# One attention kernel on one core: where the row shifts stand in front of the scores

## The chip, the cores and the metric

The kernel runs on one core of one Trainium2 chip. Its time is the device time of the whole launch in microseconds (us). Before the change it is 4384.06 us, the median of three runs that lie between 4382.21 and 4387.28.

## What is computed

The input x has 4 sequences of 2048 tokens with 512 features. Two branches work on the layer-normalised x, and both are added to x.

```python
xn  = layernorm(x)
qkv = xn @ w_qkv                       # 16 heads of 32
q, k = irfft(rfft(q) * mask), irfft(rfft(k) * mask)
out = softmax(q @ k.T / sqrt(32)) @ v  # per sequence and head
y1  = out @ w_out + b_out
y2  = top-1 experts: 8 experts with 100 places each, one shared weight w_expert
return x + y1 + y2
```

The attention branch is nearly all of the work. The softmax is over 2048 keys for each of 2048 queries, 16 heads and 4 sequences.

## The kernel before

**Tiling.** Four heads make a group, so there are 16 pairs of sequence and group (k in the code). Each has four blocks of 512 queries (n), and each block has 16 tiles of 128 keys (j). One tile of keys is a **half** (two of them, even and odd, make a window). There are 16 x 4 x 16 = 1024 halves. In a half the scores of four heads are computed, keys on the partitions and queries along the row, in two **rounds** u of two heads each. A head has 32 features, so its matmul takes 32 of the 128 rows of the array: round 0 uses the row groups that begin at 0 and 32, round 1 those at 64 and 96.

**The shift.** The softmax needs the maximum over the keys, which lie across partitions here. So the maximum is taken ahead of time in a second product with queries on the partitions: `max_matmuls` (line 465) multiplies q and k once more, and `max_reduce` (line 477) lets VectorE (DVE) reduce two banks to maxima. The list `stream` (line 454) orders these products 40 pieces ahead of the scores that need them; each round of a half takes one piece, always of the other two heads, so that with the scores of the round all four row groups are at work. At the end of a block the negated maxima go through a transpose (`max_close`), are split into three bf16 parts (`max_split`, GpSimd) and sent by SyncE into `negm`. `shift` (line 619) adds them up in PSUM with a matmul of three ones per head, in bf16; `scores` (line 608) then accumulates the product of keys and queries into the same bank. ScalarE (ACT) takes the exponential of each of the four banks, and in the next half `products` (line 635) multiplies the result with v, four heads side by side in the columns of the array; DVE adds that to the running sum `num`. The sums of exponentials are gathered from pairs of tiles by an accumulating transfer (`pair`) and by GpSimd (`add_to`).

**Banks.** PSUM is one array of eight banks. `bank()` (line 118) and `next(turns)` hand them out strictly in turn. A half takes nine: four for scores, four for maxima, one for `products`. Whoever gets a bank waits until the last reader of what it held is done.

**Order.** Every engine runs its instructions in the order in which the program emits them (`InOrder`, line 72, pins it). The main loop (lines 950 to 1005) emits for each half: shifts, then in each round the maximum matmuls, scores, exponentials and the reduce, then the products of the half before, then the steps that `agenda` holds for this half. The agenda is planned ahead of the loop: projections of the next pair, transposes, the router, the experts, and the closing steps of the block before (row sums, eight reciprocals, output projection). `at` (line 801) puts a step into a half and adds its planned cost on PE to `costs` (line 798), `spread` (line 805) places a list of steps so that the costs are even, and line 934 adds 0.5 where `max_close` falls. A step of DVE, ACT or GpSimd alone is planned with cost 0.

For pieces of the maximum beyond the last (the last 20 halves) the rounds hold only scores.

Of the kernel before, what the change touches and what calls it, by code (L numbers as in the profile page):

```python
# [102 lines left out]
def attention_and_top1_experts(ctx: ExitStack, tc: tile.TileContext, a: dict, out: bass.AP):  # L103
# [14 lines left out]
    def bank():  # L118

        return array[:, next(turns), :]  # L120
# [36 lines left out]
    def chunk(name):  # L157
        tag, bufs = ("y", 1) if name == "y" else ("xs", None)
        return chunks.tile([P, TQ, DM], F32, tag=tag, name=name, bufs=bufs)

    def probs(odd):

        name = "odd" if odd else "even"
        return probs_pool.tile([P, 2, 2, QB], F32, tag=name, name=name, bufs=3 if odd else 5)
# [300 lines left out]
    def max_matmuls(item, half):  # L465
        k, n, m, t, u = item
        for h in range(2):
            at = DH * (2 * u + h)
            on.tensor.matmul(
                array[:, half[h], :],  # L470
                lhsT=qs[k, n][at : at + DH, t * P : (t + 1) * P],
                rhs=ks[k][at : at + DH, m * QB : (m + 1) * QB],
                start=True,
                stop=True,
            )

    def max_reduce(item, half):
        k, n, m, t, u = item
        if (k, n) not in parts:
            parts[k, n] = small.tile([P, HG, TQ, NQ], F32, name="part", bufs=2)  # L480
        for heads, scored in joined(*half):
            part = parts[k, n][:, 2 * u : 2 * u + 2, t, m]
            on.vector.reduce_max(part[:, heads], scored, axis=AX.X)
        if (m, t, u) == (NQ - 1, TQ - 1, 0):
            full_blocks.append((k, n))
# [3 lines left out]
    def max_negate(k, n):  # L489
        negs[k, n] = small.tile([P, HG * TQ], F32, name="neg")  # L490
        part = parts.pop((k, n)).rearrange("p h t m -> p (h t) m")
        on.vector.tensor_reduce(negs[k, n], part, AX.X, ALU.max, negate=True)

    def max_close(k, n):

        pn = bank()[0 : HG * TQ, 0:P]
        on.tensor.matmul(pn, lhsT=negs.pop((k, n)), rhs=ident, start=True, stop=True)
        rest = small.tile([HG * TQ, P], F32, name="rest")
        row = small.tile([HG * TQ, 3, P], BF16, name="row", bufs=2)
        on.scalar.copy(row[:, 0, :], pn)  # L500
        on.scalar.copy(rest, pn)
        closed[k, n] = rest, row
# [3 lines left out]
    def max_split(k, n):  # L506

        rest, row = closed.pop((k, n))
        for i in (1, 2):
            on.gpsimd.tensor_tensor(rest, rest, row[:, i - 1, :], ALU.subtract)  # L510
            on.gpsimd.tensor_copy(row[:, i, :], rest)
        negms[k, n] = qkv.tile([P, QB], BF16, tag="negm", name="negm", bufs=3)
        for i in range(3):
            on.sync.dma_start(out=negms[k, n][i::DH, :], in_=row[:, i, :])
# [93 lines left out]
    def scores(k, n, j, u, half):  # L608
        for h in range(2):
            at = DH * (2 * u + h)  # L610
            on.tensor.matmul(
                half[h],
                lhsT=ks[k][at : at + DH, j * P : (j + 1) * P],
                rhs=qs[k, n][at : at + DH, :],
                start=False,
                stop=True,
            )

    def shift(k, n, u, half):
        for h in range(2):  # L620
            at = DH * (2 * u + h)
            on.tensor.matmul(
                half[h],
                lhsT=ones_b[at : at + 3, :],
                rhs=negms[k, n][at : at + 3, :],
                start=True,
                stop=False,
            )
# [6 lines left out]
    def products(k, n, j, tile, num):  # L635
        po = bank()
        four_heads(po, lambda at: vs[k][:, j, at], tile, start=True, stop=True)
        if j == 0:
            on.scalar.copy(num, po)
        else:  # L640
            on.vector.tensor_tensor(num, num, po, ALU.add)
# [156 lines left out]
    costs = [0.0] * len(agenda)  # L798
# [140 lines left out]
    def pair(first, second):  # L939
        on.gpsimd.dma_start(out=first, in_=second, accum_op=ALU.add)  # L940

    def add_to(tile, sum_before, engine):
        for u in range(2):
            engine.tensor_tensor(tile[:, u], tile[:, u], sum_before[:, u], ALU.add)
# [3 lines left out]
    window = 0  # L948
    maxima = stream[MAX_AHEAD:]
    for k in range(B * NG):  # L950
        for n in range(NQ):
            num = work.tile([P, QB], F32, tag="num", name="num")
            tiles = {}
            for w in range(NW):
                even, odd = w * WIN, w * WIN + 1
                if window in splits:
                    max_split(*splits.pop(window))
                for step in heads[2 * window]:
                    step()
                if window in pairs:  # L960
                    pair(*pairs.pop(window))
                if window in adds:
                    add_to(*adds.pop(window))
                for j in (even, odd):
                    tiles[j] = probs(j == odd)

                    halves = [(bank(), bank()) for u in range(2)]
                    for u in range(2):
                        shift(k, n, u, halves[u])
                    for u in range(2):  # L970
                        half = halves[u]

                        mate = maxima.pop(0) if maxima else None
                        if mate:
                            mh = next(turns), next(turns)
                            max_matmuls(mate, mh)
                        scores(k, n, j, u, half)
                        for h in range(2):
                            on.scalar.activation(tiles[j][:, u, h, :], half[h], AF.Exp, scale=SCALE)
                        if mate:  # L980
                            max_reduce(mate, mh)
                    while full_blocks:
                        filled = full_blocks.pop(0)
                        max_negate(*filled)
                        full[window + 1] = filled
                    if left:
                        products(*left)
                    left = k, n, j, tiles[j], num
                    if j == even and window in full:
                        splits[window + 1] = full.pop(window)  # L990
                        max_close(*splits[window + 1])
                    for step in agenda[2 * window + (j == odd)]:
                        step()
                last = (k, n) == (B * NG - 1, NQ - 1)
                if not last or w < NW - 2:
                    pairs[window + 1] = tiles[even], tiles[odd]
                    if 0 < w:

                        due, engine = (2, on.gpsimd) if maxima else (3, on.vector)
                        adds[window + due] = tiles[even], tiles[even - WIN], engine  # L1000
                if last and w == NW - 2:
                    y = chunk("xs")
                    on.sync.dma_start(out=y, in_=o[B - 1, n])
                window += 1
            ended[k, n] = num, tiles[NT - WIN]
# [39 lines left out]
```

## Time and profile before

| | us |
|---|---|
| three runs, median | 4384.06 |
| profiled execution | 4377.26 |
| its span, first to last instruction | 4375.4 |
| DVE busy | 3345.9 |
| GpSimd (POOL) busy | 2942.7 |
| ACT busy | 2653.9 |
| DVE's wait for PE before reduces of `part` | 921.0 |
| shift matmuls, mean of one | 0.385 |
| score and maximum matmuls, mean of one pass | 0.59 |

The granted TensorE clock was 0.993 over the span. All steps are recorded at one line, L83, that of the helper that pins the order, so rows are told apart by the tiles they write and read: `array<-negm,ones_b` is the shift, `array<-q,k` the scores, `array<-k,q` the maximum matmuls, `array<-even,v` and `array<-odd,v` the products, `array<-xnT,wg` a projection, `array<-wo,ot` the output projection. In a timeline row the first number is the start in us from the span's beginning, the second the length; x4 means that four instructions are merged into the row. PEld are weight loads. Each f32 matmul appears as two instructions. The ends of matmuls are modelled: they hold the way through the array as well, so that neighbours overlap in the rows, and the distance from start to start is the better measure.

### The profile page before, as it was taken

The page shows a single profiled execution, that of the slowest core. Times are in us where ns is not written, and L with a number is a line of the kernel's source. Part 1 is how long each engine was busy: PE and PEld are TensorE (multiplying, and loading weights), DVE is VectorE, ACT ScalarE, POOL GpSimd, SP SyncE. Part 2 cuts the span into 40 slices and gives each one's busy share as a digit, 9 for nine tenths or more (in the row PEclk, how much of TensorE's full clock was granted, in tenths as well). Part 3 has the DMA queues.
Part 4 walks back from the last instruction along what each step waited for, and adds up shares of the span by engine and source line. Part 5 has one row for each costly group of instructions (what it writes and reads, how often), then busy time and mean ns, then how long its engine had stood idle before and what let it go on. Part 6 is the DMA issues. An engine that isn't in the chain of part 4 may idle for free. (4 is left out here: it accounts for less than half of the span.)

```text
span 4375.4 us, 129380 instructions
## 1 busy us (share of the span) xinstructions
PE 4281.4 (98%) x56110; PEld 1906.5 (44%) x56110; DVE 3345.9 (76%) x4059; ACT 2653.9 (61%) x5527; POOL 2942.7 (67%) x2009
## 2 busy tenths in 40 slices
PE   8999999989999999999999999998999999999998
PEld 4444444434444444443544444443444443544432
DVE  6777778867777777886777877787777877677786
ACT  3556666666666666657566666665756665566665
POOL 0677666666776666776677766767668676677773
PEclk9999999999999999999999999999999999999999
DMA  4777877887777778788677777788877886778788
GB/s 116 182 140 153 158 151 164 190 186 146 141 150 154 153 152 159 168 191 184 128 156 153 154 151 154 160 173 191 165 137 153 166 165 130 142 156 162 153 158 171
DMA packets 161379, 690.71 MB, mean 158 GB/s; under 512 B 25302, under 2 KB 30584, under 8 KB 95528
## 3 DMA queue, kind: packets, MB, share of 16 engines
q0 software_dynamic: 110432, 605.83, 70.7%
q1 hardware_dynamic: 49200, 76.09, 5.6%
q8 instruction: 439, 7.19, 0.6%
q14 instruction: 132, 1.08, 0.1%
q10 hardware_dynamic: 1176, 0.52, 0.1%
HBM read 59.27 MB, written 88.96 MB: 34 GB/s over the span
## 5 line engine op out<-in xcount | busy, mean ns | idle before, releaser
L83 DVE TENSOR_REDUCE part<-array 128x2 f32<-128x1024 f32 (+1 forms) x2297 | 2427.8, 1104 | 924.4 <-PE array L83 921.0
L83 POOL TENSOR_TENSOR even<-even 128x1024 f32<-128x1024 f32 x876 | 2124.4, 2530 | 473.8 <-DMA even<-odd 473.1
L83 PE MATMUL array<-q,k 32*128 32x512 f32 x8192 | 1936.3, 593 | 0.0
L83 PE MATMUL array<-k,q 32*128 32x512 f32 x8192 | 1930.3, 591 | 2.2 <-DVE part L83 1.5
L83 ACT ACTIVATE even<-array 128x512 f32<-128x512 f32 x2048 | 1058.1, 604 | 496.0 <-PE array L83 488.2
L83 ACT ACTIVATE odd<-array 128x512 f32<-128x512 f32 x2048 | 1057.4, 603 | 485.2 <-PE array L83 387.2
L83 PEld LDWEIGHTS array<-k,q 32*128 32x128 f32 x8192 | 820.0, 187 | 423.3 <-issue 270.7
L83 POOL DMA_DIRECT2D even<-odd x510 | 468.5, 919 | 681.5 <-ACT odd L83 624.9
L83 PEld LDWEIGHTS array<-q,k 32*128 32x128 f32 x8192 | 762.5, 184 | 39.3 <-issue 17.1
L83 DVE TENSOR_TENSOR num<-num,array 128x512 f32<-128x512 f32 x960 | 649.8, 677 | 25.0 <-PE array L83 18.7
L83 PE MATMUL array<-even,v 128*32 128x512 f32 x4096 | 545.6, 605 | 14.2 <-ACT odd L83 14.2
L83 PE MATMUL array<-odd,v 128*32 128x512 f32 x4096 | 546.9, 605 | 7.4 <-ACT even L83 7.4
L83 PEld LDWEIGHTS array<-xnT,wg 128*32 128x32 f32 x15808 | 446.7, 110 | 242.5 <-issue 125.8
L83 PE MATMUL array<-xnT,wg 128*32 128x128 f32 (+1 forms) x15808 | 527.3, 277 | 0.7 <-ACT xnT L83 0.7
L83 PE MATMUL array<-negm,ones_b 3*128 3x512 bf16 x4096 | 440.7, 385 | 13.0 <-DVE num L83 7.6
L83 PEld LDWEIGHTS <-ones_b 3*128 3x128 bf16 x4096 | 111.7, 91 | 466.7 <-issue 466.7
L83 PE MATMUL array<-wo,ot 128*32 128x512 f32 x2048 | 268.9, 598 | 37.0 <-POOL ot L83 36.9
L83 PEld LDWEIGHTS array<-wg,xnT 128*32 128x32 f32 x8192 | 231.9, 110 | 124.6 <-issue 62.8
L83 DVE RECIPROCAL factor<-den 128x64 f32<-128x64 f32 x504 | 273.9, 544 | 0.0
L83 PE MATMUL array<-wg,xnT 128*32 128x128 f32 x8192 | 263.8, 273 | 0.0
L83 PEld LDWEIGHTS array<-even,v 128*32 128x32 f32 x4096 | 80.7, 108 | 408.6 <-ACT odd L83 400.4
L83 PEld LDWEIGHTS array<-odd,v 128*32 128x32 f32 x4096 | 81.0, 108 | 407.8 <-ACT even L83 398.5
(126 smaller groups left out, 1588.8 us busy)
## 6 DMA issues: line engine op xcount, KB each, us to landing
even<-odd POOLq DMA_DIRECT2D x510, 1024.0 KB, 8.1
out_dram<-y POOLq DMA_DIRECT2D x63, 1024.0 KB, 10.1
xs<-in_L_attn_x_dram SPq DMA_DIRECT2D x30, 1024.0 KB
out_dram<-xs SPq DMA_DIRECT2D x16, 1024.0 KB
wg<-wd SPq DMA_DIRECT2D x15, 768.0 KB
wo<-in_L_attn_w_out_dram SPq DMA_DIRECT2D x16, 256.0 KB
negm<-row SPq DMA_DIRECT2D x192, 4.0 KB
even<-in_L_attn_w_qkv_dram SPq DMA_DIRECT2D x2, 512.0 KB
```

The lines of the kernel that those rows point to most:

```text
L83: done = act(*args, **kwargs)
```

## The change

In a half whose predecessor holds agenda steps with a cost on PE, the shifts of both rounds stay ahead of everything, as before. In the other halves each round's two shifts are emitted at the head of that round. With them the two banks of round 1's scores are taken from the turn at that point, after the two banks of round 0's maxima, and not before them.

```diff
-                    halves = [(bank(), bank()) for u in range(2)]
-                    for u in range(2):
+
+                    together = costs[2 * window + (j == odd) - 1] > 0
+                    halves = [(bank(), bank()) for u in range(2)] if together else []
+                    for u in range(2 * together):
                         shift(k, n, u, halves[u])
                     for u in range(2):
+                        if not together:
+                            halves.append((bank(), bank()))
+                            shift(k, n, u, halves[u])
                         half = halves[u]
 
                         mate = maxima.pop(0) if maxima else None
```

So on PE the order of a half of the second kind is: two shifts, two maximum matmuls, two scores, two shifts, two maximum matmuls, two scores.

## The prediction

> **What bounds the kernel now.** I read the page's first lines first, then the waits of PE, then the timeline of single halves.
>
> ```profile
> PE 4281.4 (98%) x56110; PEld 1906.5 (44%) x56110; DVE 3345.9 (76%) x4059; ACT 2653.9 (61%) x5527; POOL 2942.7 (67%) x2009
> ```
>
> PE bounds. Only 94 us of the span of 4375.4 have no matmul in flight, but matmul ends are modelled, so a short stall inside a half does not show as idle time. Starts in the timeline do show it. This is an ordinary half, with a projection piece as its other work (PE rows alone):
>
> ```profile
> 1501.17 0.40 PE L83 MATMUL array<-negm,ones_b 3*128 3x512 bf16 x4
> 1501.40 0.59 PE L83 MATMUL array<-q,k 32*128 32x512 f32 x2
> 1501.41 0.59 PE L83 MATMUL array<-k,q 32*128 32x512 f32 x2
> ...
> 1503.23 1.06 PE L83 MATMUL array<-odd,v 128*32 128x512 f32 x8
> 1504.11 1.06 PE L83 MATMUL array<-xnT,wg 128*32 128x128 f32 x32
> 1505.10 0.39 PE L83 MATMUL array<-negm,ones_b 3*128 3x512 bf16 x4
> ```
>
> Shifts take 0.23 (start to start). Scores (q,k) and maximum matmuls (k,q) run on four row groups at once; each f32 matmul is two passes of 0.43 (the next start at 1501.83). Four passes (two rounds) end about 1503.12, 0.10 later the products start, 0.88 later the projection. A half without other work would take 0.23 + 1.72 + 0.10 + 1.0 = 3.05. Now the end of a block, where halves hold no other work:
>
> ```profile
> 625.12 0.40 PE L83 MATMUL array<-negm,ones_b 3*128 3x512 bf16 x4
> ...
> 626.46 2.36 DVE L83 TENSOR_REDUCE part<-array 128x2 f32<-128x1024 f32 x2 [0.75 <-PE array L83]
> 626.55 2.06 ACT L83 ACTIVATE odd<-array 128x512 f32<-128x512 f32 x4 [1.01 <-PE array L83]
> 627.22 1.07 PE L83 MATMUL array<-even,v 128*32 128x512 f32 x8
> 628.22 0.84 PE L83 MATMUL array<-negm,ones_b 3*128 3x512 bf16 x4
> 628.67 0.09 PEld L83 LDWEIGHTS <-ones_b 3*128 3x128 bf16 x1 [0.35 <-issue]
> ...
> 628.90 1.09 PE L83 MATMUL array<-k,q 32*128 32x512 f32 x3
> ...
> 630.79 1.07 PE L83 MATMUL array<-odd,v 128*32 128x512 f32 x8
> 631.79 0.85 PE L83 MATMUL array<-negm,ones_b 3*128 3x512 bf16 x4
> ```
>
> The half at 625.12 takes 3.10, the one at 628.22 takes 3.57. Its first two shifts start at 628.22; the third only at 628.67, when the last of ACT's four exponentials (626.55 + 2.06 = 628.61) has freed its bank; scores and maxima start at 628.88, when DVE's second reduce (626.46 + 2.36 = 628.82) has freed the next. Without these waits they would start at 628.45: 0.43 lost, and 0.1 more because weight loads come late (a score matmul shows 0.69 in place of 0.59). The half at 631.79 repeats it.
>
> **The change, part by part.** It adds and removes no instruction on PE. From the planned costs I count 83 of 1024 halves whose predecessor has cost 0: only these split their shifts. 36 follow a half that still leads with all four (a first split half: that at 628.22), 47 follow another split one (a later: that at 631.79). All others keep their order.
>
> Banks: a half takes nine of eight in turn, so each place takes the bank that the next place held one half earlier. Now, the order is S0 S0 S1 S1 M0 M0 M1 M1 P (scores, maxima of either round, products), and the opening shifts wait for all four exponentials and a reduce, the first maxima for the last reduce. Split, it is S0 S0 M0 M0 S1 S1 M1 M1 P.
>
> First split half: after a leading half, M0's first bank is the one that S1's last exponential frees: 628.67. Queued behind that wait is the score pair of round 0, so it starts there too. The chain of the row groups 64 and 96 is then 628.67 + 0.10 (weights no longer loaded behind a shift) + 0.86 maxima + 0.21 shift + 0.86 scores = 630.70. Before, the products at 630.79 say 630.69. So **0 us**; ends -0.1 (weights hidden after all) and +0.1.
>
> Later split half, at 631.79: nothing that opens it waits any more (the third exponential is done by 631.5: round 1's scores start at 629.84, their second pass 0.43 later, and 0.72 after that, as for 629.41 and 630.13 in the trace, ACT can start). 631.79 + 0.01 + 0.10 + 0.86 = 632.76; shift to 632.97. A new last wait comes: M1's second bank holds the products of 630.79, and DVE adds them 1.51 later (627.22 to 628.73), at 632.30, done about 632.98. Round 1's scores are queued behind this wait. 632.98 + 0.10 + 0.86 + 0.10 drain = products at 634.05, against 634.36 in the trace: **0.30 saved**; ends 0.2 and 0.45 (the add hidden).
>
> Later split halves in a row, where DVE also has a reciprocal each half: its own work is 2.27 (two reduces) + 0.59 (add) + 0.56 (reciprocal) = 3.42, against periods of 3.48 to 3.61 now. DVE is next: **0.13 saved**; ends 0 and 0.2.
>
> Count of the 47: 19 of the first kind (14 block ends, 4 before row sums, 1 early), 17 with reciprocals, 3 where the half then stands for 11 us behind POOL's chain at a stage change (PE's waits on POOL `ot` reach 11.1), 8 in the tail without maxima. The last two kinds give 0: there the banks and matmuls are the same, in another queue order. Sum: 19 x 0.30 + 17 x 0.13 = **7.9 us**.
>
> The queues of ACT, POOL and SP keep their order; DVE gets 8 fewer split reduces (two of 683 for one of 1220: 1.2 us in all, hidden). The last halves of a block have DVE, ACT and POOL free enough: POOL's two adds and pair transfer take about 5.9 of a 6.8 us window. If that cover is gone, a pair landing late holds an ACT tile, and the 7.9 shrinks.
>
> **A rule that speaks against it.** The Trainium skill (TensorE: Matmul & The Clock Gate, Part 3, What overlaps and what doesn't) says that matmuls start and end strictly in program order, only weight loads being pulled ahead, and those only into another row group. Then the second shift pair would stand behind the second pass of the scores ahead of it: in the 11 split halves without maxima up to 0.64 each, 7 us; and its weight load, into a row group still at work, 0.09 in each of 83, 7.5 us. The change would gain nothing. The trace disagrees twice. At 1501.40 the scores start before the maxima, which are ahead of them in the program: rows 0 and 32 came free first. And here a shift in one pair of row groups runs beside scores in the other:
>
> ```profile
> 4160.64 0.09 PEld L83 LDWEIGHTS <-ones_b 3*128 3x128 bf16 x1 [0.35 <-issue]
> ...
> 4160.66 0.70 PE L83 MATMUL array<-q,k 32*128 32x512 f32 x2
> ...
> 4160.86 0.61 PE L83 MATMUL array<-k,q 32*128 32x512 f32 x2
> ```
>
> The second shift pair started at 4160.64, scores on the other rows at 4160.66, maxima on the shift's own rows 0.22 after it. bf16 and f32 mix and the row groups queue apart. I take the row: 0. Not shown anywhere is a bf16 weight load while f32 matmuls stream; the nearest row is an f32 load at 1501.83 into rows whose second pass had just begun, at no cost.
>
> **The rivals.**
> - Whole relief: the add is never late and loads stay hidden. 28 first halves x 0.5 + 19 x 0.5 + 17 x 0.15 = 26 us, 4358. Against it: the banks above, counted by hand.
> - Absorbed: waits of ACT tiles on pair transfers (18.0 us now), DVE or tail take it back: 4384, within 4 of it. For it: two halves of the tail take 5.25 and 9.44 where 2.18 is usual, held by DVE and transfers.
> - Slower: the bf16 weight load in mid-half cannot run beside f32 matmuls and drains the row groups. Place: the second shift pair of all 83. Price: 0.2 in 36 later halves, 0.15 in 33 first ones, 1.1 in 11 without maxima (half of it absorbed by stalls there): 7 + 5 + 6 to 13, less 7.9, is 10 to 17 slower, about 4396. It decides once a split half pays over 7.9 / 83 = 0.095. For it: now all 4096 loads of ones_b stand where nothing else runs; against it: 628.22, where three such loads overlap running shifts.
> - That the order does not change can be excluded: the built program shows the moved shifts.
>
> **Numbers.** The profiled execution took 4377.26 (span 4375.4), 6.8 below the median of three, 4384.06; the sum of waits saved is taken off either: 4369.4 profiled, 4376.2 for the median. Chances: forecast 0.58 (4372 to 4381), whole relief 0.09, absorbed 0.13, slower 0.20. 0.2% (8.8 us) is about what a measurement can tell from no change; the forecast lies just inside, so 0.27 of its 0.58 is faster. Faster 0.36, same 0.44, slower 0.20. The range 4368 to 4396 leaves out whole relief and half of slower.
>
> **What will tell.** Right: first split halves stay at 3.57, later ones take about 3.27 (3.42 with reciprocals), their second shift pair starting 0.9 to 1.0 after the first while scores run, and the DVE add ending just before the last maximum. Wrong: first split halves near 3.1 (whole relief); a pause before the second shift pair, with longer halves in the tail (slower); shorter halves at an unchanged total (absorbed).

## The result, and the profile after

The changed kernel takes 4376.22 us (median of 18 runs, 4371.10 to 4379.97), the kernel before 4383.86 us (18 runs, 4380.91 to 4387.41). The ratio is 0.9981, 95% interval 0.9974 to 0.9987: about 8 us faster, real, and just below the 0.2% that the prediction took as its bound. The profiled execution took 4371.16 us (before 4377.26), its span is 4369.4 us (before 4375.4), at the same granted clock of 0.993. So the total is the predicted one. The terms of its sum are not, as the halves below show.

The busy times of the engines, from the top of the page of the changed kernel:

```profile
PE 4279.1 (98%) x56110; PEld 1911.6 (44%) x56110; DVE 3344.5 (77%) x4051; ACT 2658.5 (61%) x5527; POOL 2942.0 (67%) x2009
```

This line hardly tells the two kernels apart: PE has the same 56110 matmuls and is 2.3 us less busy, and DVE has 4051 instructions where it had 4059, the 8 split reduces less that were forecast. What changed is where matmuls start. This is the end of the same block as in the prediction, from the timeline of the changed kernel (start in us, length, engine, operation; the bracket is the idle time before it and what ended it):

```profile
626.35 0.39 PE L83 MATMUL array<-negm,ones_b 3*128 3x512 bf16 x2
626.79 0.19 PEld L83 LDWEIGHTS array<-k,q 32*128 32x128 f32 x2 [0.35 <-ACT odd L83]
...
627.75 0.38 PE L83 MATMUL array<-negm,ones_b 3*128 3x512 bf16 x2
...
628.93 1.06 PE L83 MATMUL array<-odd,v 128*32 128x512 f32 x8
...
629.92 0.39 PE L83 MATMUL array<-negm,ones_b 3*128 3x512 bf16 x2
...
630.26 0.68 DVE L83 TENSOR_TENSOR num<-num,array 128x512 f32<-128x512 f32 x1
630.46 0.59 PE L83 MATMUL array<-k,q 32*128 32x512 f32 x2
630.46 0.10 PEld L83 LDWEIGHTS <-ones_b 3*128 3x128 bf16 x2
...
630.89 0.38 PE L83 MATMUL array<-negm,ones_b 3*128 3x512 bf16 x2
630.99 0.18 PEld L83 LDWEIGHTS array<-k,q 32*128 32x128 f32 x1 [0.22 <-DVE num L83]
...
631.01 0.67 PE L83 MATMUL array<-k,q 32*128 32x512 f32 x2
...
632.07 1.07 PE L83 MATMUL array<-even,v 128*32 128x512 f32 x8
...
633.92 0.39 PE L83 MATMUL array<-negm,ones_b 3*128 3x512 bf16 x4
```

The half at 626.35 is a first split half. Its two opening shifts start at once, and then the maxima wait 0.44 for a bank that ACT's last exponential frees (626.79). It takes 3.57 to the next half, as before. The half at 629.92 is a later one. Nothing waits at its head; its second shift pair starts 0.97 after the first, while scores and maxima of round 0 run. The one wait left is that of round 1's maxima for DVE's add of the products (630.26, released at 630.99). It takes 4.00, output piece included, where the same half took 4.43 before.

I measured all 1024 halves in this way, from the first shift of one to the first shift of the next, in both profiled executions. Positive is saved, and a split half is "first" or "later" as in the prediction:

| halves | number | predicted, us | measured, us | each (measured) |
|---|---|---|---|---|
| first split, with maxima | 33 | 0 | +1.0 | median -0.01 |
| later split | 19 | 5.7 | +8.1 | mean +0.43 |
| later split, with a reciprocal each | 17 | 2.2 | +4.8 | mean +0.28 |
| later split, stage change | 3 | 0 | +0.7 | mixed |
| split, tail without maxima | 11 | 0 | -4.5 | one of them -6.6 |
| all that still lead, and the prologue | 941 | 0 | -4.1 | singly within 1.2 |
| sum | | 7.9 | 6.0 | |

The rows of split halves repeat in other traces. The row of the 941 others does not: up to half 976, where three of the kernels below (e5, e8, e10) are the same as the changed one, the halves that lead are between 3.2 us slower (changed kernel) and 1.4 faster (e5) than in the one trace of the kernel before, with the prologue counted in. So most of its -4.1 is scatter between executions (1.2 of it is half 1008, below).

Up to the end of half 1003 the changed kernel is 11.4 us ahead, after half 1006 12.0, after half 1007 only 5.4, and at the end 6.0. Half 1007 (counted from 0) is one in which PE comes to the output projection of the block before, and that needs `ot` from POOL. PE's timeline there, with the shifts of half 1008, of the changed kernel and then of the kernel before:

```profile
4295.88 1.93 PE L83 MATMUL array<-wo,ot 128*32 128x512 f32 x8 [4.84 <-POOL ot L83]
4297.75 0.61 PE L83 MATMUL array<-negm,ones_b 3*128 3x512 bf16 x4
```

```profile
4302.16 1.06 PE L83 MATMUL array<-wo,ot 128*32 128x512 f32 x8 [0.53 <-POOL ot L83]
4303.16 0.40 PE L83 MATMUL array<-negm,ones_b 3*128 3x512 bf16 x4
```

PE stood 4.84 us for it, in place of 0.53. Over the whole span PE's wait on `ot` grew from 36.9 to 41.1 us. The rows show a second cost: behind the stall the same eight matmuls take 1.87 to the next shift, and 1.00 before. The clock says why. These are the engines' busy times over halves 992 to 1007, changed kernel and then before; the third number from the end of a line is the granted TensorE clock:

```profile
4238.49:4297.75 59.26, 54.26 (x463) 18.53 (x461) 44.06 (x54) 36.91 (x72) 43.10 (x29) 0.96 0.83 163
```

```profile
4248.24:4303.16 54.92, 53.92 (x462) 18.29 (x459) 42.70 (x52) 36.70 (x72) 39.13 (x28) 1.00 0.82 160
```

In the changed kernel's trace the granted clock is 0.50 from 4293.4 to 4300.2, which covers the end of half 1007 and most of half 1008 (4.19 in place of 3.04). Of the 7.7 us that these two halves lose, 4.3 are the longer wait for `ot`, 2.0 the matmuls at half the clock behind it, and 1.4 lie ahead of it, where ACT waits 1.60 for a tile that POOL's add still holds (4287.88). So in these two executions the change won about 12 us and gave about 6 of them back in one place.

### The profile page after: what moved, and what is told of

It reads as the page before. It is cut to its first block, busy times and chain, and to the rows that moved or that the text cites. A ratio compares the mean times of both kernels' runs of the same rounds, so it can differ in the third digit from the quotient of the medians.

```text
span 4369.4 us, 129421 instructions
## 1 busy us (share of the span) xinstructions
PE 4279.1 (98%) x56110; PEld 1911.6 (44%) x56110; DVE 3344.5 (77%) x4051; ACT 2658.5 (61%) x5527; POOL 2942.0 (67%) x2009
## 3 DMA queue, kind: packets, MB, share of 16 engines
q14 instruction: 133, 1.09, 0.1%
## 5 line engine op out<-in xcount | busy, mean ns | idle before, releaser
L83 PE MATMUL array<-wo,ot 128*32 128x512 f32 x2048 | 269.7, 600 | 41.2 <-POOL ot L83 41.1
```

What stands on the lines that cost most here:

```text
L83: done = act(*args, **kwargs)
```

## The experiments

All twelve are variants of the changed kernel, each timed in five rounds against the kernel before on the same chip; a ratio is to that. The chips differ from run to run, so kernels are compared by ratios. "Cost" of a half in the code is the planned cost of its agenda steps on PE.

### The order of the queue alone, and the order of the banks alone

The first kernel keeps the split emission but takes all four score banks ahead of it, in the old order. The second takes the banks in the new order but emits all four shifts ahead.

```diff
 # e1_order_only
-                    halves = [(bank(), bank()) for u in range(2)] if together else []
+                    halves = [(bank(), bank()) for u in range(2)]
...
-                            halves.append((bank(), bank()))
                             shift(k, n, u, halves[u])
 # e2_banks_only
-                    for u in range(2 * together):
+                    halves = [(bank(), bank())]
+                    early_mh = None
+                    if not together and maxima:
+                        early_mh = next(turns), next(turns)
+                    halves.append((bank(), bank()))
+                    for u in range(2):
                         shift(k, n, u, halves[u])
```

> Splits the shifts in the same 83 halves, but all four score banks are taken up front as before the change. Theory (the gain comes from the bank order): with the old order the second bank of the first maxima is still the one that DVE's last reduce frees (0.65 after the half's natural start), and now round 0's scores and round 1's shifts queue behind it, so each of the 69 split halves with maxima is some 0.2 longer than before the change: about 14 us slower, 4398 where the kernel before has 4384. Rival (the gain comes from the queue order, the second shift pair no longer standing in front): as the change, about 8 us faster, 4376.

> All four shifts lead in every half as before the change; only the banks are handed out in the order of the change (round 0's scores, round 0's maxima, round 1's scores, round 1's maxima) in the 83 halves. Theory (it needs both, bank order and queue order): the fourth shift now waits for DVE's last reduce, so later split halves stay at about 3.6 and the first ones grow by up to 0.2; total between the kernel before and 14 us slower, 4384 to 4398. Rival (bank order alone is enough): about 8 us faster, 4376.

Measured: order alone 4378.92 us, ratio 1.0002 (0.9993 to 1.0010); banks alone 4381.47 us, ratio 1.0009 (1.0001 to 1.0018). With the order alone first split halves became 0.21 longer (3.57 to 3.78), 4.8 us in all. Of the 19 later ones an extra 0.2 was expected too; 8 of them kept their length (4.43 mostly), 10 became 0.20 to 0.34 shorter (4.40 to 4.20 mostly) and one longer, together 2.1 us saved. With the banks alone the two kinds became 0.10 and 0.11 longer. So neither part gains anything in the total. The full gain of a later half needs both: the shift of round 1 must stand behind round 0 in the queue, and round 0's maxima must get the banks that come free early. That moving the shifts alone brings the gain is refuted by the first kernel, though it relieves half of the later halves in part; that the bank turn alone does is refuted by the second.

### Which bank holds the first split halves

The prediction's step for them was that M0's first bank (M0 are the maxima of round 0, S1 the scores of round 1) is the one of S1's last exponential. In this kernel a first split half gives the fourth and fifth bank of its turn to M0, the third and sixth to S1; all else is the change.

```diff
+                    here = 2 * window + (j == odd)
+                    swap = here > 1 and not together and costs[here - 2] > 0 and len(maxima) > 1
...
+                    if swap:
+                        halves.append((bank(), bank()))
+                        b3, b4, b5, b6 = (next(turns) for _ in range(4))
+                        early_mh = b4, b5
+                        halves.append((array[:, b3, :], array[:, b6, :]))
```

> As the change, but in each split half that follows a leading one round 0's maxima take the fourth and fifth bank and round 1's scores the third and sixth, so that the first maxima no longer wait for the bank of the last exponential. Theory (that bank is why these 33 halves saved nothing): they fall from 3.58 to about 3.15, and 25 to 28 of them keep it, so 10 to 12 us more than the change: about 4365. Rival (they are held by something else, DVE's reduce or weight loads): they stay at 3.58 and the time at 4376.

Measured: 4360.42 us, ratio 0.9963 (0.9949 to 0.9976), 17.5 us off the span of before. The first split half of the same block in this kernel's timeline:

```profile
626.12 0.39 PE L83 MATMUL array<-negm,ones_b 3*128 3x512 bf16 x2
626.12 0.70 PE L83 MATMUL array<-k,q 32*128 32x512 f32 x2
...
628.42 1.06 PE L83 MATMUL array<-odd,v 128*32 128x512 f32 x8
629.42 0.39 PE L83 MATMUL array<-negm,ones_b 3*128 3x512 bf16 x2
```

The maxima start with the shifts, 0.44 earlier than in the changed kernel, and the half takes 3.30 in place of 3.57. So that bank did hold it. Part of the 0.44 comes back at once: the maxima of round 1 now wait (627.21, 0.13 behind the shift), and the later half that follows saves 0.31 in place of 0.43.

### The price of a split where nothing is gained

Every half splits its shifts, so 941 more than in the change.

```diff
-                    together = costs[2 * window + (j == odd) - 1] > 0
+                    together = False
```

> Every half splits its shifts, whatever the half ahead of it holds. Theory (in a split half the first maxima start with a weight load of 0.10 that no shift covers, and nothing is won where other work gives the banks time): some 900 halves pay 0.10 each, 80 to 100 us slower, 4465 to 4485, while the 33 first split halves become later ones and win 10. Rival (the load is hidden, splitting is free and helps every half): at most 4376, or lower.

Measured: 4420.76 us, ratio 1.0100 (1.0085 to 1.0116), about 43 us slower than before and half of the 80 to 100 expected. Halves that hold a piece of cost 1 became 0.083 longer (642 of them), of cost 2 0.093 (189), without a wait to relieve. A half with a projection piece, as in the prediction's first window, from this kernel's timeline:

```profile
1516.51 0.39 PE L83 MATMUL array<-negm,ones_b 3*128 3x512 bf16 x2
1516.51 0.70 PE L83 MATMUL array<-k,q 32*128 32x512 f32 x2
...
1517.04 0.59 PE L83 MATMUL array<-k,q 32*128 32x512 f32 x2
...
1518.65 1.06 PE L83 MATMUL array<-odd,v 128*32 128x512 f32 x8
```

From the first shift to the products it is 2.14, against 2.06 for the half at 1501.17 before. The first maxima start at once but show 0.70 in place of 0.59: their f32 weight load now has no shift in front of it to hide behind. Their second passes start 0.53 behind the first (1517.04), where 0.43 is usual, and this 0.10 makes up the price; a pause at the bf16 weight load, which the rival "slower" needs, does not show. In the profiled execution the halves that led before cost 56 us in all up to the tail (less than 932 times 0.083, since some others of them became shorter), and the first split halves save 0.40 each, 13 us: their predecessor, split too, no longer leaves the late bank.

### Splitting also the half ahead, and leading again near the end

Three kernels put the last run of short halves back (all halves from 998 on lead), to see whether that run starves POOL and makes half 1007 long: the change, the swap of banks, and a split of every half that holds no work or follows one that holds none.

```diff
 # e5_not_last
-                    together = costs[2 * window + (j == odd) - 1] > 0
+                    together = costs[2 * window + (j == odd) - 1] > 0 or 2 * window >= 998
 # e6_swap_not_last: the swap of e3, and
+                    together = costs[here - 1] > 0 or here >= 998
 # e7_either_not_last
+                    here = 2 * window + (j == odd)
+                    together = (costs[here - 1] > 0 and costs[here] > 0) or here >= 998
```

> As the change, but from half 998 on all four shifts lead again, as before the change. Up to there the change had saved 10.1 us by half starts; behind it the half at which the output projection waits for POOL's `ot` lost 6.6 of it. Theory (the shorter halves of the last run leave POOL no time for its adds, so the gain is given back): that half takes 3.8 us again and the total is about 10 us below the kernel before, ratio 0.9977. Rival (that half is late by the chance of a transfer's landing, whatever the order): some 6 us are lost there all the same, ratio 0.9990 or above.

> The third run's exchange of banks in first split halves, with all shifts leading from half 998 on. Theory: the third run had saved 22 us by half 998 and lost 5 behind it; those are kept now, ratio 0.9950 (about 22 us). Rival: the tail takes its 5 us in any case, ratio 0.9963 as in the third run.

> Shifts split where the half itself or the one ahead of it holds no other work, banks in turn, all leading from half 998 on. Theory (a half that is split pays 0.08 for its uncovered weight load where the banks were free anyway, and then every half behind it is a later one): the former first halves fall to 3.16, the halves newly split grow by at most 0.1, together 0.35 per pair more than the change, 10 to 20 us below the kernel before in all, ratio 0.9955 to 0.9975. Rival (the newly split halves lose what the first ones win): as the change, 0.998.

Measured: 4369.30 us, ratio 0.9980 (0.9973 to 0.9987); 4360.97 us, 0.9965 (0.9951 to 0.9979); 4362.97 us, 0.9966 (0.9954 to 0.9979). In the first of them halves 999 to 1003 are back at 3.57, but half 1007 still takes 9.31 (10.42 in the change, 3.85 before). With the swap it takes 9.63, in the third 5.49. So the length of the last run's halves does not make half 1007 long, and this theory falls. The third kernel confirms the other step: with their predecessor split, the first split halves save 0.43 each (median), and that predecessor pays 0.03.

### POOL's adds near the end

Two kernels leave work out: the four adds that POOL makes for sums of exponentials at halves 1000 and 1002 (e8), or at halves 984 and 986 (e10). The row sums of one block of queries are then incomplete. If POOL's queue is simply too full there, half 1007 must shrink.

```diff
 # e8_fewer_adds; e10_fewer_adds_early has (492, 493)
-                    add_to(*adds.pop(window))
+                    late = adds.pop(window)
+                    if window not in (500, 501):
+                        add_to(*late)
```

> The change with POOL's four adds of the windows at halves 1000 and 1002 left out, so the row sums of one query block lack some tiles; all else is the same. Theory (POOL comes late to the last output projections because of the adds queued ahead): the half at 1007 falls from 10.4 to about 4 us, and the total is about 12 us below the kernel before, ratio 0.9973. Rival (the half waits for a transfer, not for POOL's queue): it stays near 10, ratio 0.998 to 0.999.

> The change with POOL's four adds of the windows at halves 984 and 986 left out, so row sums of one query block lack some tiles. Theory (POOL's lag comes from that run): the half at 1007 falls from about 10.5 to at most 5.5 us, 976 to the end takes at most 184 us, ratio about 0.997. Rival (not POOL's queue but the transfers themselves): 1007 stays near 10, 976 to the end at 187 or more, ratio 0.998 to 0.999.

Measured: 4369.65 us, ratio 0.9982 (0.9975 to 0.9988), half 1007 at 11.28; and 4370.61 us, ratio 0.9979 (0.9970 to 0.9988), half 1007 at 10.22. It did not shrink. POOL merely waited for transfers instead of adding. So POOL's own work is not what makes `ot` late.

### Leading earlier, and moving the output transfer

The swap again, with all halves from 976 on leading (e9); and the swap with the output transfer `out_dram<-y`, which POOL also issues, put two halves later in the two blocks ahead of the tail (e12).

```diff
 # e9_swap_976
+                    together = costs[here - 1] > 0 or here >= 976
 # e12_swap_later_output
-        return steps + [(first + TQ - 1 + first % 2, 0, add)], (first - first % 2, divide)
+        wait = 2 if (k, n) in ((B * NG - 2, NQ - 1), (B * NG - 1, 0)) else 0
+        return steps + [(first + TQ - 1 + first % 2 + wait, 0, add)], (first - first % 2, divide)
```

> The exchange of banks in first split halves, with all shifts leading again from half 976 on, so that the last two block ends before the tail run as before the change. Theory now (POOL falls behind already in the run at 984 to 988, whose halves are 0.3 shorter, then issues the output transfer late, and the pair transfers behind it land late): from half 976 to the end it takes the 185.9 us of the kernel before, and all that was saved ahead of it, about 20 us, is kept: ratio 0.9955. Rival (the tail takes its 5 us however the run ahead of it goes): 187.5 to 189 us from 976 on, ratio 0.9965.

> The exchange of banks in first split halves, and in the two blocks ahead of the tail the output transfer of `y` is issued two halves later, behind the next pair transfer and not in front of it. In all runs so far the half at 1007 took at most 5.5 us where that transfer was issued in half 995, and 8.7 to 11.3 where POOL came to it only in half 996, just ahead of the pair transfer. Theory (the pair transfer then queues behind the output's 1 MB, lands late, and POOL's adds and `ot` behind it): the half at 1007 takes at most 5.5 us, 976 to the end at most 184, ratio about 0.9955. Rival (POOL or the transfers are late in any case once halves are shorter): 1007 stays at 9 to 11, 976 to the end at 187, ratio 0.9963 as in the third run.

Measured: 4359.35 us, ratio 0.9957 (0.9944 to 0.9971); and 4364.49 us, ratio 0.9957 (0.9943 to 0.9970). With halves 984 to 1003 exactly as long as before, half 1007 still takes 8.69: what makes it long is already there at half 976. With the transfer moved it takes 9.23. The adds next to it came earlier, but a later pair transfer landed late in its place. This theory falls too.

What these kernels do show is where POOL loses its time. POOL's timeline of the changed kernel, and then that of the kernel before, at the same place in the program:

```profile
4255.00 1.29 POOL L83 DMA_DIRECT2D out_dram<-y  x1
4255.80 1.41 POOL L83 DMA_DIRECT2D even<-odd  x1
4260.70 0.85 POOL L83 DMA_DIRECT2D even<-odd  x1 [3.50 <-ACT odd L83]
4269.74 4.68 POOL L83 TENSOR_TENSOR even<-even 128x1024 f32<-128x1024 f32 x2 [8.20 <-DMA even<-odd]
```

```profile
4261.12 1.63 POOL L83 DMA_DIRECT2D out_dram<-y  x1
4264.26 0.87 POOL L83 DMA_DIRECT2D even<-odd  x1 [1.51 <-ACT odd L83]
4270.83 0.85 POOL L83 DMA_DIRECT2D even<-odd  x1 [5.69 <-ACT odd L83]
4275.39 4.66 POOL L83 TENSOR_TENSOR even<-even 128x1024 f32<-128x1024 f32 x2 [3.71 <-DMA even<-odd]
```

Before, the output transfer is issued 3.1 ahead of the pair transfer, in half 995; in the changed kernel 0.8 ahead, in half 996, because POOL comes to it later against PE and ACT, and the tile of the pair is ready by then. The add that needs that pair transfer starts 13.9 us after its issue (the transfer's own semaphore says 13.8; 8.1 is the median of all), POOL stood 8.20 in place of 3.71, and from there to `ot` (4294.58) it has one gap of 2.44 and else none to make it up. In every kernel but e12, half 1007 is short (3.85 to 5.5) where the output transfer is issued in half 995 and long (8.7 to 11.3) where it is issued in half 996. e12 is long without that.

The traces say more than these times. A pair transfer as late as this one is common: in the changed kernel 16 of 62 are issued 0.8 behind an output transfer and land 13.8 to 17.3 after their issue, in the kernel before 14, which land 13.9 to 18.9; those 2.6 behind it land after 12 to 13 in both, but for one of 16.3. So a late transfer is not what is new at half 1007. From the issue of the output transfer to the end of `ot`, POOL's chain of transfers and adds takes 40.99 us before and 40.83 in the changed kernel (39.2 to 42.0 in all fourteen traces). PE comes to the output projection 40.52 after that issue before, and 36.04 after it in the changed kernel. The chain has not become longer; PE reaches its end 4.5 sooner, and the wait is the difference. Of the 4.5, halves 999 to 1004 account for 1.8; the rest is that POOL issues the output transfer later in PE's course. e9 shows that this lag does not need shorter halves behind 976. Where it arises stays open, and no run shortened the chain.

The gap between short and long is widened by the clock. In the nine traces in which PE waits 4.6 us or more for `ot` there, the granted clock falls to 0.50 for 6.8 us and half 1008 takes 3.87 to 4.56; in the five in which it waits 2.2 or less, it does not fall and half 1008 takes 3.04.

### DVE as the bound of runs with reciprocals

The change with four reciprocals of 128 columns for eight of 64. A wide one takes 0.94, a narrow one 0.54. If DVE bounds these halves, those that hold a wide one must become longer, and those that no longer hold any shorter.

```diff
-PART = 64
+PART = 128
```

> The change with four reciprocals of 128 columns per block in place of eight of 64. Theory (in the runs of halves with reciprocals DVE bounds at 3.26, its reduces, add and reciprocal back to back): later split halves with a wide reciprocal take about 3.5 (0.3 more work in one half), those behind them without one 3.14; halves 856 to 858 and 1000 to 1003 show it. Rival (PE's own chain through the add sets 3.26): all stay at 3.26. The total is within 3 us of the change either way, ratio 0.997 to 0.999.

Measured: 4368.15 us, ratio 0.9978 (0.9969 to 0.9987). Halves in which DVE has a wide reciprocal take 3.66 in place of 3.26 (0.40 more, the difference of 0.94 and 0.54; about 3.5 was expected). DVE's timeline in the changed kernel, then in this one:

```profile
4155.60 2.29 DVE L83 TENSOR_REDUCE part<-array 128x2 f32<-128x1024 f32 x2
4157.80 0.67 DVE L83 TENSOR_TENSOR num<-num,array 128x512 f32<-128x512 f32 x1
4158.39 0.54 DVE L83 RECIPROCAL factor<-den 128x64 f32<-128x64 f32 x1
4158.86 2.28 DVE L83 TENSOR_REDUCE part<-array 128x2 f32<-128x1024 f32 x2
```

```profile
4152.68 2.29 DVE L83 TENSOR_REDUCE part<-array 128x2 f32<-128x1024 f32 x2
4154.88 0.68 DVE L83 TENSOR_TENSOR num<-num,array 128x512 f32<-128x512 f32 x1
4155.48 0.94 DVE L83 RECIPROCAL factor<-den 128x128 f32<-128x128 f32 x1
4156.34 2.28 DVE L83 TENSOR_REDUCE part<-array 128x2 f32<-128x1024 f32 x2
```

In both DVE goes from one half's reduces to the next without a gap: 3.26 from 4155.60 to 4158.86, and 3.66 from 4152.68 to 4156.34. The half follows DVE to the hundredth. The halves just behind, now without a reciprocal, became shorter: half 972 3.49 in place of 3.78. The 17 halves of runs with reciprocals give back the 4.8 us that they had gained, and yet the total is that of the change: half 1007 takes 5.26 here and the clock stays up.

## Why the prediction was right, and which of its terms were not

**The total: right, by errors that cancel.** 4376.2 was predicted and 4376.22 measured. That is luck. The split halves with maxima saved 14.5 us in the profiled execution and not 7.9 (1.0, 8.1, 4.8 and 0.7 by kind), of which scatter in the others leaves 12 up to half 1007 (14 to 15 in e5, e8 and e10), and the tail took about 6 back where the forecast had 0.

**First split halves, 0 saved: right.** They measure 3.57 before and after. The step was the bank of S1's last exponential, and e3 shows it: give M0 another bank, and the wait of 0.44 at its head is gone. The working had products 2.57 behind the first shift (628.22 to 630.79), the run has 2.58.

**Later split halves, 0.30 saved: mechanism right, size too small.** Second shifts start 0.97 after the first, as worked out. The last wait is the one named, M1's second bank and DVE's add. The term that failed is "DVE adds them 1.51 later". That distance came from a half in which DVE's add stood behind reduces that had themselves started late. In the split half the maxima are ready sooner, and the add starts 1.33 behind the products (628.93 to 630.26). So M1 starts 1.09 after the half's start and not 1.29, the products 2.15 after it and not 2.26; 0.30 and these 0.11 make the measured 0.43 nearly whole.

**Runs with reciprocals, 0.13 saved: mechanism right, size too small.** DVE is the bound, e11 shows it. The term that failed is the 3.42 of its own work. It was added up from distances in the kernel before, where DVE was not yet the bound (0.56 for a reciprocal, 2.27 for the reduces). When DVE runs without a gap the same instructions follow each other in 2.20, 0.59 and 0.47: 3.26. From 3.57 that is 0.31 for most of them, 0.28 as a mean.

**Tail, 0: wrong by about 6.** "There the banks and matmuls are the same, in another queue order" held for the split halves themselves: most of the eleven are within 0.02, half 1004 saved 0.43, half 1012 1.9. But half 1007 lost 6.6, and 1008 1.2 behind it. The prediction had named the cover (POOL 5.9 of a 6.8 window, "a pair landing late"), and let it hold. It did not: POOL's chain to `ot` kept its 41 us while PE came 4.5 sooner, and the stall also cost 2.0 at half the clock, a term that the forecast did not have. Taking away the last run of short halves (e5), some of POOL's adds (e8, e10) or moving the output transfer (e12) did not help, so why POOL lags there stays open.

**The rule that spoke against it: refuted here.** By the Trainium skill (TensorE: Matmul & The Clock Gate, Part 3, What overlaps and what doesn't) matmuls start strictly in program order; then the second shift pair would stand behind the scores in front of it. In eight of the eleven tail halves without maxima it starts 0.020 after the first pair. Half 1006 of the changed kernel, in which the program has two scores between the pairs:

```profile
4285.13 0.41 PE L83 MATMUL array<-negm,ones_b 3*128 3x512 bf16 x4
...
4285.36 1.04 PE L83 MATMUL array<-q,k 32*128 32x512 f32 x8
```

All four shifts run ahead of all scores. And the bf16 load among f32 matmuls, which no trace had shown, is the row at 630.46 above: it lies beside maxima and scores without a pause, so the slower rival (0.2 a half) falls. The small real price is that of e4: 0.083 a half where the first f32 weight load loses its cover. In the split halves it is paid too, inside what they save.

**The other rivals.** "Whole relief" (4358) did not come, for the reason given: the first split halves keep their bank. With the swap (e3, e9, e12), which lets them go, about two thirds of it come: ratios of 0.9957 to 0.9963, 16 to 19 us of the 26. "Absorbed" happened by half: about 6 of 12. Five versions have lower ratios than the change (e3, e6, e7, e9, e12). Only the intervals of e9 and e12 lie clear of the change's; e9, the swap with leading halves from 976 on, is 0.9957 (0.9944 to 0.9971), some 19 us below the kernel before.

## What to carry to other kernels

When buffers rotate strictly in turn, write down which old holder each place waits for under the new order, half by half: that told here which halves would gain and which would not, and one swap of two banks doubled the gain. Take the distance of a wait from a row in which the engine stood for the same reason; a distance measured where it was late for another reason, or had slack, mis-sizes the term (1.51 for 1.33, 3.42 for 3.26). And when a bound engine gets faster, look for the place where another queue had just enough cover: here a chain of 41 us that did not shorten with it took half of the gain, a part of it through the clock that fell during the stall.

## What the runs showed of the hardware

- Row groups queue apart also between bf16 and f32: the second pair of shifts starts 0.020 us after the first (eight tail halves), though it stands behind the scores of the other row groups in the program; a bf16 weight load of 0.10 lies beside running f32 matmuls (630.46).
- The first f32 matmul after the products shows 0.70 in place of 0.59 when no shift in its own rows is ahead of it, and a half then costs 0.083 more (e4).
- DVE without a gap needs 3.26 from start to start for two reduces, an add and a reciprocal, where the distances in a looser queue add up to 3.42.
- A pair transfer (1 MB, accumulating) issued 0.8 us behind an output transfer landed 13.8 to 17.3 us after its issue (16 of them in the changed kernel), where 8.1 is the median of all; issued 2.6 behind it, after 12 to 13, but for one.
- Behind a PE wait of 4.6 to 7.2 us the granted clock was 0.50 for 6.8 us in nine traces, and eight matmuls took 1.87 in place of 1.00 (changed kernel); behind waits of 2.2 us or less, in five traces, it did not fall.
